# Attention plus a spectral layer on one core: folding the spectral weights by column, and reordering the start of the kernel

## The chip, the core and the metric

The kernel runs on one core of a Trainium2 chip. A core has five engines that run their own instruction queues in order: TensorE (PE, matrix multiply; PEld is its weight load), VectorE (DVE), ScalarE (ACT), GpSimd (POOL) and SyncE (SP, which here only issues DMAs). PE writes to PSUM banks, and DVE or ACT carry results from there to SBUF; POOL works on SBUF alone. The metric is the device time of one launch in microseconds, and lower is better.

## What is computed

For x of shape (2, 2048, 256), with xn = layernorm(x):

```
out = x + attention(xn) + spectral(xn) + bias
attention: q = xn@wq (16 heads of 16), k, v = xn@wk, xn@wv (4 heads), rotary on q and k,
           causal softmax(q k^T / 4) v, then @wo
spectral:  real(ifft(fft(xn) @ (w_re + i w_im)))       along the 256 features
```

The spectral layer is linear in xn, so the kernel works it out as one 256x256 matrix, called mff, and adds xn @ mff. With C and S the cosine and sine tables (dft[0], dft[1]) mff is a sum of products of the form C·(w·C), S·(w·S) and so on, divided by 256.

## The kernel before, in words

Work is cut into 8 blocks n of 512 rows: for each of four row ranges j one block of each of the two batch rows, so that blocks 0 and 1 have j = 0, blocks 2 and 3 have j = 1, and so on. Every block goes through the same chain.

1. `load_x` (L166) loads the block by one 512 KB DMA from SP's queue into one of two buffers xt. Block 0's is issued first, then the rotary table `trig` (L180), then block 1's (L181). The projection weights come by ACT's queue.
2. `row_stats` (L233, DVE, four times), `row_power` (L241, POOL: rstd), `row_shift` (L247, DVE: -mean*rstd), and `norm` (L398), which scales and shifts in place: on DVE for block 0, on POOL for all others.
3. `transpose_x` (L405): PE transposes through a PSUM bank, and ACT copies to xnT. `features` (L419) multiplies by the projection weights, once for keys and values (c = NK) and twice for the queries (c = 0, 1), each time two terms k into one bank, which ACT copies to `raw` (L427). `other_half` gives the swapped halves for the rotary turn.
4. `rotate` and `split` (L514, L531) turn the rows and split them into three bf16 parts, seven operations for each c: on DVE for block 0, on POOL for the others. SP's DMAs then stack the parts into `qst` (queries) and `kst` (keys).
5. For each of the block's four head groups (a "unit"): the exact row maxima, by PE products `sm` and DVE's TENSOR_REDUCE `mx` (L636), the so-called A work; the scores again, transposed, `st` (L743), with ACT's exponential `es` (L745), the B work; and the values `av` (L780), the V work. A unit's scores need its maxima, which `parts` and `spread` (L644, L668) put into `qst` by a small DMA from ACT's queue.
6. `output` (L895) adds xnT @ mff and attT @ wo in a bank, and DVE adds x and the bias.

`rotary_table` (L276) widens the rotary table for a range j by eight DVE operations (L293, tile trx) and turns it by eight PE transposes (L305, ps_tr). `spectral_matrix` (L315) makes mff: four results `left` (two column halves o, for "at" and "et", bank ps_ff), each a sum of four 256-wide products, and two results `right` (bank ps_mff) of four products each, after ACT has negated the sine table (L320). `product` (L151) issues one product as four matmuls, each for 32 columns of the weights; a float32 one shows as eight records. Its inputs are loaded on POOL's queue by `load_late` (L217).

Nothing runs by priority on the chip: each engine takes its instructions in the order in which the program was written out, and that order comes from a planner in the same file (L919 to L1203). It keeps a modelled clock for each engine (`use` and `send` add costs to it), a table `there` of when each value or buffer slot is ready, and lists ("streams") of pieces, each with a first step, a due step, an engine, the things it needs and the slots it takes. A step is one 128-key tile of B work for one unit. The loop at L1096 takes the earliest piece of the other engines while it is due before PE's next, and otherwise picks PE work: A when late, then a forced piece (F: its due step has come), then B, A, V, and a piece that isn't due yet (M) last. A slot in a ring (three PSUM banks "st", three "raw", eight "es", ...) is taken in turn, and work that needs a slot waits until the user three (or eight) turns before has released it.

The start is written by hand (L963 to L977): 48 transposes of an identity keep PE busy (L968, tile idle), DVE fills the constant tiles of block 0, then row_stats, row_power, load_late, row_shift and the ordering of the weights on ACT. `chain` (L979) puts a block's pieces into streams, with first steps taken from when the block's A work is due; within the PE stream the k-th piece of a later block may start at step `s["pe"] + k // 2`.

Of the kernel before, what the change touches and what calls it, by code (L numbers as in the profile page):

```python
# [10 lines left out]
F32 = mybir.dt.float32  # L11
# [6 lines left out]
P = 128  # L18
# [5 lines left out]
def tile_attn_plus_spectral_ffn(  # L24
# [79 lines left out]
    def slot(tag, more=0):  # L104

        return tag, used[tag] + more - ring[tag]
# [57 lines left out]
    xt = {}  # L164

    def load_x(n):  # L166
        send("sp", 512, [slot("xt")], [("xt", "in", n)])
        take_slot("xt")
        xt[n] = work.tile([P, NI, D], F32, tag="xt", bufs=2, name=f"xt{n}")
        nc.sync.dma_start(out=xt[n], in_=block_rows(n))  # L170

    take_slot("qst"), take_slot("qst")
    load_x(0)
# [43 lines left out]
    def load_late():  # L217

        for name, src, tag, bufs in (
            ("wre", w_re, "inv", 2), ("dc", dft[0], "inv", 2),  # L220
            ("wim", w_im, "attT", 2), ("ds", dft[1], "avs", 3),
        ):
            take_slot(tag)
            spec[name] = work.tile([P, NK, D], F32, tag=tag, bufs=bufs, name=name)
            nc.gpsimd.dma_start(out=spec[name], in_=src.rearrange("(c p) n -> p c n", p=P))
            send("pool", 256, (), ["spec"])
        nc.gpsimd.dma_start(out=wo_sb, in_=wo.rearrange("(c p) n -> p c n", p=P))
        nc.gpsimd.dma_start(out=bias_sb, in_=bias.partition_broadcast(P))

# [3 lines left out]
    def row_stats(n, i):  # L233
        if i == 0:
            mv[n] = work.tile([P, NI, 2], F32, tag="mv", bufs=2, name=f"mv{n}")
        st = work.tile([P, 6], F32, tag="bn", bufs=3, name=f"bn{n}_{i}")
        nc.vector.bn_stats(st, xt[n][:, i, :])
        nc.vector.bn_aggr(mv[n][:, i, :], st)
        use("dve", 0.53, [("xt", "in", n)], [("mv", n)])

    def row_power(n):  # L241
        rstd[n] = work.tile([P, NI], F32, tag="rs", bufs=2, name=f"rs{n}")
# [3 lines left out]

    def row_shift(n):  # L247
        shift[n] = work.tile([P, NI], F32, tag="sh", bufs=2, name=f"sh{n}")
        nc.vector.scalar_tensor_tensor(
            shift[n], mv[n][:, :, 0], -1.0, rstd[n], ALU.mult, ALU.mult  # L250
        )
        use("dve", 0.2, [("rs", n)], [("sh", n)])

# [20 lines left out]
    def rotary_table(j):  # L276
        ex = []

        def expand():
            at = []  # L280
            for a in range(2):
                ex.append(work.tile([P, NI, P], F32, tag="raw", bufs=3, name=f"trx{j}_{a}"))
                at.append(slot("raw"))
                take_slot("raw")
            for f in range(2):
                for a, e, k in ((0, 0, 0), (0, 1, 0), (1, 0, 2), (1, 1, 1)):
                    cols = f * HP + e * QD
                    wide = (
                        trig[:, j * NI : (j + 1) * NI, k, :]
                        .unsqueeze(3)  # L290
                        .to_broadcast([P, NI, HALF, NKV])
                    )
                    nc.vector.tensor_reduce(  # L293
                        ex[a][:, :, cols : cols + QD].rearrange("p i (d h) -> p i d h", h=NKV),
                        wide.unsqueeze(4), AX.X, ALU.max,
                    )
            use("dve", 1.15, at, [("trx", j)])
            there["trx slots", j] = used["raw"]

        def turn(a):  # L300
# [9 lines left out]
        return expand, turn  # L310


    mff = const.tile([P, NK, D], F32, name="mff")

    def spectral_matrix():  # L315
        wre, wim, dc, ds_ = (spec[k] for k in ("wre", "wim", "dc", "ds"))
        neg_s = work.tile([P, NK, D], F32, tag="xr", bufs=3, name="neg_s")
        at_ = work.tile([P, NK, D], F32, tag="xr", bufs=3, name="at_")
        et_ = work.tile([P, NK, D], F32, tag="xr", bufs=3, name="et_")
        nc.scalar.mul(neg_s, ds_, -1.0)  # L320
        use("act", 0.48, ["spec"], ["neg_s"])
        first_xr = used["xr"]
        for _ in range(3):
            take_slot("xr")
        pieces = []

        def left(o, name, dst, parts):
            cols = slice(o * P, (o + 1) * P)
            ps = bank(f"ps_ff{o}")[:, :D]
            for a, (w, f) in enumerate(parts):  # L330
                for c in range(NK):
                    product(
                        ps, w[:, c, cols], f[:, c, :],
                        start=(a == 0 and c == 0), stop=(a == 1 and c == NK - 1),
                    )
            nc.scalar.mul(dst[:, o, :], ps, 1.0 / D)
            through_bank(1.87, ["neg_s"], "act", 0.29, [("left", o, name)])

        def right(r):
            cols = slice(r * P, (r + 1) * P)  # L340
            ps = bank(f"ps_mff{r}")[:, :D]
            for a, (w, f) in enumerate(((at_, dc), (et_, neg_s))):
                for c in range(NK):
                    product(
                        ps, w[:, c, cols], f[:, c, :],
                        start=(a == 0 and c == 0), stop=(a == 1 and c == NK - 1),
                    )
            nc.scalar.copy(mff[:, r, :], ps)
            lefts = [("left", o, name) for o in range(NK) for name in ("at", "et")]
            through_bank(1.87, lefts, "act", 0.29, [("mff", r)])  # L350
            if r == NK - 1:
                for tag, k in (
                    ("inv", 0), ("inv", 1), ("attT", 0), ("avs", 0),
                    ("xr", first_xr), ("xr", first_xr + 1), ("xr", first_xr + 2),
                ):
                    there[tag, k] = clock["pe"]

        for o in range(NK):
            pieces.append((["neg_s"], lambda o=o: left(o, "at", at_, ((wre, dc), (wim, ds_)))))
            pieces.append((["neg_s"], lambda o=o: left(o, "et", et_, ((wim, dc), (wre, neg_s)))))  # L360
        lefts = [("left", o, name) for o in range(NK) for name in ("at", "et")]
        for r in range(NK):
            pieces.append((lefts, lambda r=r: right(r)))
        return pieces

# [11 lines left out]
    def project(n):  # L379
# [2 lines left out]
        b, j = blocks[n]  # L382
        e, eng = (nc.vector, "dve") if n == 0 else (nc.gpsimd, "pool")
        MULT, SUB, CAST, NORM = (0.72, 0.72, 0.46, 0.33) if n == 0 else (1.23, 1.13, 0.63, 0.53)
        raw, sw, swp, part, ra, at = {}, {}, {}, {}, {}, {}
        sends = []
        streams.append(sends)

# [27 lines left out]
            if c == NK - 1:  # L416
                there["xt", n] = clock["pe"]

        def features(c):  # L419
            ps = bank(f"ps_q{n}_{c}")  # L420
            for k in range(NK):
                product(
                    ps, wp[:, k, c, :], xnT[n][:, k, :], start=(k == 0), stop=(k == NK - 1)
                )
            raw[c] = work.tile([P, SB], F32, tag="raw", bufs=3, name=f"raw{n}_{c}")
            at[c] = take_slot("raw")
            nc.scalar.copy(raw[c], ps)  # L427
            through_bank(
                1.83, ["wp", *(("xnT", n, k) for k in range(NK))], "act", 0.48, [("raw", "in", n, c)],
                [("raw", at[c] - ring["raw"])],  # L430
            )
            if n >= 2:
                other_half(c)
# [134 lines left out]
        ]  # L568
        for c in (NK, 0, 1):
            table = [("cs", j, 1)] * (n >= 2)  # L570
            pe.append(("pe", ["wp", *table, *xs], ["st", "raw"] + ["sw"] * (n >= 2), lambda c=c: features(c)))
            if n < 2:
                pe.append(("pe", [("raw", "in", n, c)], ["st", "sw"], lambda c=c: other_half(c)))
            if c == NK:
                pe.append(("pe", [("raw", "in", n, NK), ("ones", n)], ["st"], proj_v))
# [397 lines left out]
        row_stats(0, i)  # L973
    row_power(0)
    load_late()
    row_shift(0)
    order_weights()  # L977

    def chain(n, starts, late=0):  # L979

        norms, pe, rot = project(n)
        eng = norms[0][0]
        stats = [("dve", [("xt", "in", n)], [], lambda i=i: row_stats(n, i)) for i in range(NI)]
        stats.append(("pool", [("mv", n)], [], lambda: row_power(n)))
        stats.append(("dve", [("rs", n)], [], lambda: row_shift(n)))
        s = starts
        if n > 1:
            stream([("sp", [], ["xt"], lambda: load_x(n))], s["load"], s["load"])
# [13 lines left out]
                out_rot.append((at, at + late + 2 + k // 2, *p))  # L1002

    def table(j, since):
        expand, turn = rotary_table(j)
        last = [("cs used", at_block[B - 1, j - 2])] if j >= 2 else []
        stream(
            [("dve", last, ["raw", "raw2"], expand)]
            + [("pe", [("trx", j)], ["st"], lambda a=a: turn(a)) for a in range(2)],
            since, since + 3,  # L1010
        )
# [4 lines left out]
    chain(1, early, 1)  # L1016
    load_x_2 = stream([("sp", [], ["xt"], lambda: load_x(2))])

    def spectral():
        for needs, piece in spectral_matrix():  # L1020
            spectral_pieces.append((-1, 8, "pe", needs, ["st"], piece))

    spectral_pieces = stream([("act", ["spec"], [], spectral)], -1, 8)
    for n in range(2, NB):
        at = next(k for k, d in enumerate(due) if d >= a_from[NG * n])
        starts = dict(load=at - 30, stats=at - 24, pe=at - 20, rot=at - 17)
# [228 lines left out]
```

## Time and profile before

| what | us |
|---|---|
| median of 3 runs (925.45 to 928.35) | 925.58 |
| the profiled execution's own time | 926.44 |
| its span, first to last instruction | 924.7 |
| PE busy | 904.6 |
| DVE busy | 748.0 |
| ACT busy | 653.7 |
| POOL busy | 370.1 |

The profile is of one execution. "Busy" is the time in which at least one instruction of the engine ran; a matmul's end is modelled, so PE's figure is somewhat generous. A timeline row gives the start, the time (of several instructions, merged, if it ends in xN), engine, line, operation, tiles and shapes, and in brackets how long the engine had been idle and what released it. The chain is the path of work and waits that ended last. A table by stage gives, for each stretch of time, its length and then the busy time of PE, PEld, DVE, ACT and POOL, with instruction counts, the clock granted to PE (1.00 is full), the share of the DMA engines and GB/s.

### The profile page before, as it was taken

What the parts mean: (1) busy time and instruction counts of PE and PEld (TensorE: products, weight loads), DVE (VectorE), ACT (ScalarE), POOL (GpSimd) and SP (SyncE); (2) the same over time, 40 slices, a digit from 0 to 9 for tenths busy, and PEclk for the clock granted to TensorE, in tenths of its full rate; (3) what the DMA queues carried; (4) which work ended last, traced back from release to release, by engine and by line L of the source; (5) the groups of instructions that cost most, each with busy time, mean ns of one, the idle gap of its engine ahead of it and who ended that gap; (6) DMA issues with size and microseconds to landing.
All of it is one profiled execution on the core that took longest, in us unless ns stands there. A gap on an engine that the chain in (4) does not pass through costs nothing.

```text
span 924.7 us, 38985 instructions
## 1 busy us (share of the span) xinstructions
PE 904.6 (98%) x17324; PEld 500.5 (54%) x17324; DVE 748.0 (81%) x1056; ACT 653.7 (71%) x1375; POOL 370.1 (40%) x556
## 2 busy tenths in 40 slices
PE   7999899999999999999999999999999999999997
PEld 4666565655555555555555555555455554645443
DVE  6878697789789996998995999979789988788601
ACT  3266565587757784888865777857688878588784
POOL 7298666824672424822236520311572021102111
PEclk9999999999999999999999999999999999999999
DMA  5435823341244011440002500010133001100000
GB/s 165 119 90 143 199 92 106 97 132 38 65 121 124 27 38 34 112 129 26 14 27 85 150 28 13 27 60 14 31 109 88 15 3 38 49 14 15 27 1 24
DMA packets 41992, 62.13 MB, mean 67 GB/s; under 512 B 8840, under 2 KB 32120, under 8 KB 41824
## 3 DMA queue, kind: packets, MB, share of 16 engines
q1 hardware_dynamic: 32400, 41.18, 16.5%
q0 software_dynamic: 8128, 17.69, 5.9%
q8 instruction: 135, 2.21, 1.0%
q10 hardware_dynamic: 1296, 0.79, 0.3%
q14 instruction: 33, 0.27, 0.1%
HBM read 32.75 MB, written 18.40 MB: 55 GB/s over the span
## 4 chain that ended last, share of the span: by engine, by line
PE 89%; DVE 5%; ACT 3%; issue 1%; DMA 1%; POOL 1%; ACTq 0%; SPq 0%; DVEq 0%; POOLq 0%
PE av L780 24%; PE st L155 22%; PE sm L155 17%; PE sm L631 7%; PE po L155 6%; PE ps_q L155 4%; DVE mx L636 2%; PE sp L155 2%; PE sm L627 2%; PE st L738 2%; ACT es L745 1%; PE ps_x L411 1%; PE st L734 1%; ACT es L747 1%; PE ps_m L671 0%
## 5 line engine op out<-in xcount | busy, mean ns | idle before, releaser
L636 DVE TENSOR_REDUCE mx<-sm 128x2 f32<-128x1024 f32 (+3 forms) x640 | 648.9, 1057 | 87.4 <-PE sm L631 44.1
L745 ACT ACTIVATE es<-st 128x512 f32<-128x512 f32 (+3 forms) x1194 | 552.4, 543 | 179.2 <-PE st L155 145.6
L155 PE MATMUL st<-qst,kst 115*32 115x512 bf16 (+3 forms) x4264 | 327.2, 354 | 1.1 <-ACT es L745 0.4
L780 PE MATMUL av<-es,va 128*32 128x512 f32 (+3 forms) x2560 | 299.9, 529 | 0.6 <-issue 0.3
L155 PE MATMUL sm<-kst,qst 112*32 112x512 bf16 x3072 | 239.1, 379 | 0.1
L155 PEld LDWEIGHTS <-kst 115*32 115x32 bf16 x4608 | 161.1, 95 | 140.6 <-issue 64.8
L752 POOL TENSOR_SCALAR_AFFINE_SELECT es<-es 128x256 f32<-128x256 f32 x192 | 76.7, 406 | 276.0 <-ACT es L745 234.8
L155 PEld LDWEIGHTS <-qst 112*32 112x32 bf16 x3072 | 96.0, 96 | 93.0 <-issue 64.8
L631 PE MATMUL sm<-kst,qst 112*32 112x32 bf16 (+15 forms) x2048 | 122.3, 281 | 0.3 <-issue 0.3
L627 PE MATMUL sm<-mask,ident_h 128*32 128x128 bf16 (+3 forms) x2048 | 100.2, 201 | 1.8 <-DVE mx L636 1.0
L780 PEld LDWEIGHTS av<-es,va 128*32 128x32 f32 x2560 | 85.1, 109 | 28.6 <-ACT avs L791 2.6
L631 PEld LDWEIGHTS <-qst 112*32 112x32 bf16 x2048 | 66.3, 97 | 34.3 <-issue 20.6
L627 PEld LDWEIGHTS <-ident_h 128*32 128x32 bf16 x2048 | 66.1, 96 | 32.2 <-issue 25.5
L906 DVE TENSOR_TENSOR xr<-po,xr 128x256 f32<-128x256 f32 x36 | 15.2, 424 | 51.5 <-PE po L155 49.5
L803 POOL DMA_DIRECT2D res<-avs x30 | 18.2, 606 | 82.7 <-ACT avs L791 79.9
L155 PE MATMUL ps_q<-xnT,wp 128*32 128x512 f32 x384 | 45.4, 600 | 0.0
L747 ACT ACTIVATE es<-sp 128x1024 f32<-128x1024 f32 (+3 forms) x43 | 36.6, 907 | 7.6 <-PE sp L155 7.4
L427 ACT COPY raw<-ps_q 128x512 f32<-128x512 f32 x24 | 14.1, 585 | 35.0 <-PE ps_q L155 35.0
L518 POOL TENSOR_TENSOR ra<-raw,cs 128x512 f32<-128x512 f32 (+1 forms) x21 | 27.4, 1304 | 24.2 <-ACT raw L427 23.0
L738 PE MATMUL st<-qst,kst 115*32 115x480 bf16 (+15 forms) x512 | 36.8, 284 | 0.1
L155 PE MATMUL po<-wo_sb,attT 128*32 128x256 f32 x512 | 34.4, 379 | 0.7 <-ACT attT L869 0.7
L155 PE MATMUL po<-mff,xnT 128*32 128x256 f32 x512 | 34.4, 380 | 0.0
(108 smaller groups left out, 657.0 us busy)
## 6 DMA issues: line engine op xcount, KB each, us to landing
qst<-run SPq DMA_DIRECT2D x62, 128.0 KB
res<-avs POOLq DMA_DIRECT2D x30, 256.0 KB, 3.0
run<-part SPq DMA_DIRECT2D x31, 192.0 KB
qst<-run SPq DMA_DIRECT2D x31, 192.0 KB
xt<-in_L_attn_x_dram SPq DMA_DIRECT2D x8, 512.0 KB
xr<-in_L_attn_x_dram SPq DMA_DIRECT2D x16, 256.0 KB
out_dram<-xr SPq DMA_DIRECT2D x16, 256.0 KB
sw<-raw SPq DMA_DIRECT2D x60, 64.0 KB
```

Source lines behind the costliest of these rows:

```text
L155: nc.tensor.matmul(to[q : q + QD], lhsT[:, q : q + QD], rhs, start=start, stop=stop)
L518: e.tensor_tensor(ra[c][:r], raw[c][:r], cs[j][:r, 0, :], ALU.mult)
L627: nc.tensor.matmul(to[:, at:wd], ident_h[:, q : q + QD], mask[:, q:], start=True, stop=True, skip_group_check=True,)
L631: nc.tensor.matmul(to[:, : at + QD], rows[:, q : q + QD], keys[:, : at + QD], start=False, stop=True, skip_group_check=True,)
L636: nc.vector.tensor_reduce(t["mx"][:, i, 2 * pr : 2 * pr + 2, k], ps[0][:, :, :wd], AX.X, ALU.max)
L738: nc.tensor.matmul(to[:, at:], keys[:, q : q + QD], rows[:, at:], start=False, stop=True, skip_group_check=True,)
L745: nc.scalar.activation(es[u, t, pr][:, e, lo:], ps[:, lo:], AF.Exp, scale=SCALE)
L747: nc.scalar.activation(es[u, t, pr][:, :, lo:], wide[pr][:, :, lo:], AF.Exp, scale=SCALE)
L752: nc.gpsimd.affine_select(out=es[u, t, pr][:, :, lo : lo + P], in_=es[u, t, pr][:, :, lo : lo + P], pattern=[[0, 2], [1, P]], compare_op=A ...
L780: nc.tensor.matmul(av[u][QD * h : QD * (h + 1), lo:], va[at_block[b, t // NI]][:, t % NI, h, :], es[u, t, h // 2][:, h % 2, lo:], start=(t ...
L803: nc.gpsimd.dma_start(out=res[n, c][f], in_=avs[u])
L906: nc.vector.tensor_tensor(xr[n, r][:, e, :], po, xr[n, r][:, e, :], ALU.add)
```

## The change

- **Loads.** Block 0 is loaded by four DMAs of 128 KB, one for each 128 rows, so that each row_stats waits for its own; other blocks as before.
- **Table.** The widening of the rotary table for j = 0 is issued on DVE between row_stats and row_shift of block 0, where it had come after row_shift.
- **Shift.** row_shift of blocks 1 to 7 goes from one DVE operation to two POOL operations.
- **Spectral weights.** Columns d and 256-d of w_re and w_im are first added or subtracted: six POOL operations ("folds"), four of them over 2x127 elements per partition, the operand for column 256-d read backwards; two copy the columns 0 and 128. Each `left` is then one sum of four products for a column half (issued in two pieces of two products), and each `right` is two products, one of them with a table `half_sb` of cosine row 128 and sine rows 1 to 127, which two more POOL DMAs load into a slot of the "es" ring. ACT's negation is gone.
- **Projections.** `features` is issued in two pieces, one for each k, between which the planner may put other PE work; the bank is held from the first to the copy after the second.
- **Planner's costs.** row_stats 0.53 to 0.6, the widening of the table 1.15 to 1.6.

```
     def load_x(n):
...
+        step = NI if n else 1
+        for i in range(0, NI, step):
+            send("sp", 128 * step, [at], [("xt", "in", n, k) for k in range(i, i + step)])
+            nc.sync.dma_start(out=xt[n][:, i : i + step, :], in_=block_rows(n)[:, i : i + step, :])
...
+        take_slot("es")
+        half_sb = spec["half"] = work.tile([P, D], F32, tag="es", bufs=ES, name="half_sb")
+        nc.gpsimd.dma_start(out=half_sb[0:1], in_=dft[0, P : P + 1, :])
+        nc.gpsimd.dma_start(out=half_sb[1:P], in_=dft[1, 1:P, :])
...
     def row_shift(n):
...
+            nc.gpsimd.tensor_scalar(shift[n], mv[n][:, :, 0], -1.0, None, ALU.mult)
+            nc.gpsimd.tensor_tensor(shift[n], shift[n], rstd[n], ALU.mult)
+            use("pool", 0.4, [("rs", n)], [("sh", n)])
...
     def spectral_matrix():
...
-        nc.scalar.mul(neg_s, ds_, -1.0)
...
+        up, down, far = slice(1, P), slice(D - 1, P, -1), slice(P + 1, D)
...
+        def fold(to, cols, one, two, op, last=False):
+            def go():
+                pool.tensor_tensor(to[:, :, cols], one, two, op)
...
+        def ends_of(to, w):
+            pool.tensor_copy(to[:, :, 0:D:P], w[:, :, 0:D:P])
...
+        folds += [lambda: ends_of(of_c, wre), lambda: ends_of(of_s, wim)]
+        fold(of_c, up, wre[:, :, up], wre[:, :, down], ALU.add)
+        fold(of_s, up, wim[:, :, up], wim[:, :, down], ALU.add)
+        fold(of_c, far, wim[:, :, down], wim[:, :, up], ALU.subtract)
+        fold(of_s, far, wre[:, :, up], wre[:, :, down], ALU.subtract, True)
+
+        def left(o, a):
+            v, f = ((of_c, dc), (of_s, ds_))[a]
...
+            for c in range(NK):
+                product(
+                    ps, v[:, c, o * P : (o + 1) * P], f[:, c, :],
+                    start=(a == 0 and c == 0), stop=(a == 1 and c == NK - 1),
+                )
...
         def right(r):
-            for a, (w, f) in enumerate(((at_, dc), (et_, neg_s))):
-                for c in range(NK):
...
+            for c, f in enumerate((dc[:, 0, :], half_sb)):
+                product(
+                    ps, left_sb[:, c, r * P : (r + 1) * P], f,
+                    start=(c == 0), stop=(c == NK - 1),
+                )
...
-        def features(c):
+        def features(c, k):
+            if k == 0:
+                held[c] = bank(f"ps_q{n}_{c}"), take_slot("st")
+            ps, at_st = held[c]
+            product(ps, wp[:, k, c, :], xnT[n][:, k, :], start=(k == 0), stop=(k == NK - 1))
...
-            pe.append(("pe", ["wp", *table, *xs], ["st", "raw"] + ["sw"] * (n >= 2), lambda c=c: features(c)))
+            pe.append(("pe", ["wp", *table, xs[0]], ["st", "raw"] + ["sw"] * (n >= 2), lambda c=c: features(c, 0)))
+            pe.append(("pe", [xs[1]], [], lambda c=c: features(c, 1)))
...
     row_power(0)
     load_late()
+    table_0 = rotary_table(0)
+    table_0[0]()
     row_shift(0)
     order_weights()
...
-        stats.append(("dve", [("rs", n)], [], lambda: row_shift(n)))
+        stats.append(("pool", [("rs", n)], [], lambda: row_shift(n)))
...
-    spectral_pieces = stream([("act", ["spec"], [], spectral)], -1, 8)
+    folds, products = spectral_matrix()
+    stream([("pool", ["spec"], [], fold) for fold in folds], -1, 4)
+    stream([("pe", *piece) for piece in products], -1, 8)
```

## The prediction, made before the changed kernel ran

> **What bounds the kernel now.** I read the page's engine table first, then a table by stage in steps of 4 us, then the chain, then the timelines of the stage that the change touches.
>
> ```profile
> span 924.7 us, 38985 instructions
> PE 904.6 (98%) x17324; PEld 500.5 (54%) x17324; DVE 748.0 (81%) x1056; ACT 653.7 (71%) x1375; POOL 370.1 (40%) x556
> ```
>
> PE is busy for all but 20.1 us. So the end moves for two reasons only: PE gets less to do, or its idle time changes. The table by stage tells where that idle time lies (second number: PE's busy time of 4.00; third from the end: granted clock):
>
> ```profile
> 8.00:12.00 4.00, 2.09 (x16) 1.48 (x13) 3.02 (x12) 2.47 (x7) 4.00 (x5) 0.97 0.32 88
> 12.00:16.00 4.00, 4.00 (x23) 1.64 (x23) 2.50 (x10) 1.30 (x3) 3.88 (x9) 0.61 0.87 261
> 16.00:20.00 4.00, 3.28 (x32) 0.90 (x28) 2.40 (x4) 0.96 (x2) 3.76 (x8) 1.00 0.43 147
> 20.00:24.00 4.00, 3.29 (x36) 1.02 (x36) 3.76 (x7) 1.16 (x3) 2.75 (x6) 1.00 0.20 67
> ...
> 104.00:108.00 4.00, 1.76 (x55) 1.37 (x58) 1.55 (x2) 1.13 (x5) 3.89 (x4) 0.91 0.37 121
> 108.00:112.00 4.00, 4.00 (x100) 3.35 (x95) 2.85 (x3) 2.11 (x4) 2.13 (x3) 0.66 0.87 233
> ```
>
> About 5 us are lost before 24 us, and 2.2 us in one gap near 105 us. In both places some 3.4 us at half clock follow ((0.03+0.39) x 4 / 0.5 and (0.09+0.34) x 4 / 0.5). The chain, in order of time, shows what PE stands behind (start, time, what):
>
> ```profile
> 29.80 2.76 DMA run<-part
> 32.58 2.74 DMA qst<-run
> 35.33 2.69 POOL xt L399 x5
> 38.06 0.33 PE ps_x L411
> ...
> 104.68 2.19 issue
> ```
>
> Block 1's norm (POOL xt L399) is on the chain, though its data came in the first 10 us. The timelines of POOL and DVE say why:
>
> ```profile
> 8.98 0.16 DVE L249 SCALAR_TENSOR_TENSOR sh<-mv,rs 128x4 f32<-128x4 f32 x1 [1.51 <-POOL rs L244]
> 9.06 1.63 DVE L293 TENSOR_REDUCE trx<-trig 128x128 f32<-128x128 f32 x8
> 18.85 1.26 POOL L244 TENSOR_TENSOR rs<-rs,neg_half 128x4 f32<-128x4 f32 x1
> 33.81 0.15 DVE L249 SCALAR_TENSOR_TENSOR sh<-mv,rs 128x4 f32<-128x4 f32 x1
> 34.78 4.30 POOL L399 TENSOR_SCALAR xt<-xt,rs,sh 128x256 f32<-128x256 f32 x8
> ```
>
> Block 1's rstd is ready at 20.1 us. Its shift stands in DVE's queue behind all of block 0's rotation and block 2's statistics, until 33.8, so the norms of blocks 1 and 2 run at 34.8 to 39.1. Meanwhile PE has the spectral products:
>
> ```profile
> 23.70 1.05 PE L155 MATMUL ps_ff<-dc,wre 128*32 128x256 f32 x16
> 24.56 1.05 PE L155 MATMUL ps_ff<-ds,wim 128*32 128x256 f32 x16
> 35.41 1.13 PE L155 MATMUL ps_mff<-neg_s,et__327 128*32 128x256 f32 x16
> ```
>
> Each row of 16 is two products; from start to start it takes 0.86 us, so a product is 0.43 us.
>
> **The change, part by part.**
>
> *Spectral products.* Before: 6 sums of 4 products, 24 x 0.43 = 10.3 us of PE. After: 2 lefts of 4 and 2 rights of 2, 12 x 0.43 = 5.2 us. PE loses 5.2 us of work, and that is worth 5.2 us only if other work fills the place. In before, nothing could: block 1 was not normed. ACT also loses the negation (0.63) and two copies (0.38 each), which is worth nothing, as ACT is idle there (1.05 us busy of 28 to 32).
>
> *Shift on POOL.* Seven DVE operations of 0.15 us go; 14 small POOL ones come, at 0.24 us each (POOL's 128x4 TENSOR_SCALAR of row_power took 0.23 to 0.24): 0.5 us a block, 3.4 in all, on an engine that is 40% busy. What matters is the queue. POOL's order for block 1 becomes power, shift, norm with nothing of DVE between. Two more DMA issues (0.6 to 0.7 each, like the 0.58 of the bias) push POOL back by 1.3, the earlier start (below) pulls by 0.6: power ends at about 20.8, the shift at 21.3, four norms of 0.55 at 23.5. Block 1 can be transposed 11 to 14 us sooner. That is the filler: two transposes (about 0.6 each for four, by the steps of the chain at 39 to 42), three projections of 1.75, three swaps of 0.9, one value turn of 0.4, together 9.7 us.
>
> *Does PE stay full?* From 21 us on it has the rest of block 0 (about 2), block 1 (9.7), spectral (5.2) and the first two units' maxima (each some 2.6 by the planner's cost; the chain's pieces agree): 22 us, to about 43. The scores began at 48.9 and are then due at about 44: maxima of the first unit begin some 2.5 us sooner and lose the 1.9 us in which DVE waited for PE (8 reductions of mean 0.78 in 8.3 us). So supply and demand match to about 1 us; I count the 5.2 in full and put the failure of this among the rivals.
>
> *Folds.* POOL's 128x512 TENSOR_TENSOR takes 1.30 us (L518), so 254 elements about 0.65; no row shows an operand read backwards, so the bounds are 0.65 and twice that. Two small copies at 0.24. Sum 3.1 to 5.7 us. A rule speaks against their place: GPSIMD Engine Reference, "8. Key points", says in the Trainium skill that POOL shares its SBUF interfaces with VectorE and contends with DVE instructions that have two SBUF inputs, and block 0's rotation on DVE is just that. The row: the pow of row_power took 1.05 us with DVE idle and 1.26 at 18.85 beside such a DVE operation, while DVE's kept its 0.68. By the rule alone I would have to charge DVE's chain up to the folds' 3 us; by the row POOL pays 20% and DVE nothing. I take the row: folds of 0.8, 3.7 us in all, 23.5 to 27.2. POOL was idle from 22.8 to 33.4, so they cost nothing; without that cover they would delay block 1's rotation, which began at 44.5 and has then 14 us of room. Their inputs landed 4.0 us after the last issue at 11.3, before POOL gets there.
>
> *First loads.* Three more issues on SP at 0.5 us push the table's and block 1's DMA from 1.3 and 1.8 to about 2.8 and 3.3. They queue behind block 0's data anyway, which landed at 5.2; bounds 0 and 1.5 for the table, I take 0. The statistics can begin when DVE's memsets end (4.63) and not at 5.25: gain 0.6 at most.
>
> *Table ahead of shift.* DVE waited 1.51 us for POOL's power (row at 8.98), then spent 1.63 on the table, and only then did the norms start (10.61). Afterwards the table runs inside that wait: statistics to 6.9, table to 8.5, shift at 8.6, norms at 8.8. With the 0.6 this is 1.8 us. If the table's data were late, shift and norms would wait behind it, up to 1.5.
>
> *Clock.* PE idled 1.80 us before its first table transpose, and half clock followed. TensorE: Matmul & The Clock Gate, "Why this matters for your kernels", asks only for no idle gaps over about 3 us; by that the half clock does not come from this gap, and closing it saves nothing more. By the rows, gaps of 1.8 and 2.19 us were each followed by it, and the 0.7 us lost in 16 to 20 was not. Afterwards the transposes follow the warm-up with no gap (table ready at 8.5, warm-up to 8.55). I take the row, at 1.0 of the 1.7 us that 3.4 at half clock can cost, as PE partly waits there anyway. Against it 0.5 for a gap near 21 us, where block 1 isn't ready yet. Start in sum: 1.8 + 1.0 - 0.5 = 2.3 us.
>
> *Projections in two pieces.* No instruction is added. The bank is held longer; bounds 0 and the rival below; I take 0, since the planner itself cannot hand out more than two further banks before the second piece. The extra first steps (k // 2 up to 4 for nine pieces, where six gave 2) delay the last projection by two steps, with 12 or more to spare.
>
> **Sum.** 5.2 + 2.3 = 7.5 us off the profiled execution's 926.44: 918.9. That execution lies 0.9 over the median of the runs, so on their scale 918.1.
>
> **Rivals.**
> 1. *The work is not replaced.* PE waits for DVE's maxima between 31 and 44 us, and the start of the scores decides. For: DVE is busy 2.77 to 3.24 of 4 there, and part of the rest was waiting for PE. Against: PE's list above. Only the start's gain is left, 2.5 us: 923.
> 2. *The gap at 104.7 goes too.* It is not a wait that the profile shows: PE stops in the middle of a product. The order behind it shifts, so it may vanish or come elsewhere. Gone, it gives 2.2 + 1.7: 914. The likeliest is that this crowded stage (DMA share 0.9) keeps a gap like it.
> 3. *Slower: a bank held.* In blocks 2 to 7, 18 times, one of three banks stays with a half-done projection. Each time at most two score products then wait for ACT's 0.54 us copies: 1.1 us at worst, 0.75 taken, 13.5 in all: 932. It turns the sign over 0.3% from 0.57 us per hold. Against: ACT itself waited 145.6 us for scores, so it is seldom behind, and PE has other work.
>
> **Chances.** The forecast 0.47, rival 1 0.22, rival 2 0.24, rival 3 0.07. Within 0.3% (2.8 us) is about what a measurement of this kernel can tell from no change. Forecast, rival 2 and a third of rival 1 lie under 922.8: faster 0.79; same 0.14; slower 0.07. The range goes from below rival 2 to above rival 1, 911.5 to 924.
>
> **What would show it.** PE has 96 records fewer of ps_ff and ps_mff together (192 before); norms on DVE start near 8.8; the clock of 12 to 16 us is near 1; block 1's norm on POOL lies near 22 and not 34.8; first scores near 44; PE's idle time up to 44 under 6 us. I am wrong if PE shows gaps between 31 and 44 with the reductions in front of them, if folds take over 1.5 us or lengthen DVE's rotation, if the start of the norms waits for the table's DMA, or if the later stages lose what the first 50 us gained.

## The result, and the profile after

The changed kernel took 928.5 us (median of 22 runs, 926.42 to 932.36), the kernel before in the same comparison 926.38 (22 runs, 922.89 to 930.99): ratio 1.003, 95% interval 1.0019 to 1.0041. The forecast was 918.1. The profiled execution took 929.23 us. A single execution lies within some 5 us of the median, so a ratio below is of medians, and a profile shows where time lies in one execution. Much of this scatter goes with the clock granted to PE: of 130 runs of the kernel before in the comparisons below, the 11 at 1.000 took 923.95 us on average and the 21 at 0.994 took 929.15. The page after:

```profile
span 927.5 us, 38848 instructions
...
PE 901.9 (97%) x17228; PEld 495.2 (53%) x17228; DVE 749.8 (81%) x1049; ACT 653.0 (70%) x1372; POOL 380.7 (41%) x578
```

PE has the 96 records fewer that were forecast. Its busy time fell by 2.7 us and not by 5.2, in part because 3.4 us more of its work ran at half clock (table below), while its idle time (span minus busy) rose from 20.1 to 25.6. The table by stage tells where (columns as before; third from the end is the clock):

```profile
12.00:16.00 4.00, 3.29 (x32) 0.90 (x28) 1.92 (x5) 0.96 (x2) 3.94 (x9) 1.00 0.85 265
20.00:24.00 4.00, 1.73 (x16) 0.16 (x8) 3.76 (x7) 0.58 (x1) 3.85 (x7) 1.00 0.30 101
24.00:28.00 4.00, 1.42 (x3) 0.54 (x3) 3.84 (x5) 0.00 (x0) 3.83 (x8) 0.70 0.35 107
28.00:32.00 4.00, 3.54 (x17) 1.52 (x21) 3.42 (x8) 1.17 (x2) 3.83 (x6) 0.50 0.63 146
...
116.00:120.00 4.00, 2.73 (x64) 1.97 (x67) 1.04 (x2) 2.26 (x7) 3.10 (x7) 0.72 0.93 234
```

The half clock of 12 to 16 us is gone, as forecast. In its place stands a hole from 20 to 32 us: PE idles 2.27 + 2.58 + 0.46 = 5.3 us there (1.0 before), and half clock follows. A gap near 116 us remains. The chain of the changed kernel, in order of time, says what PE stands behind in the hole; where the chain of before had block 0's DMAs and then block 1's norm at 35.33, it now has POOL alone:

```profile
21.77 2.37 POOL kst L413 x4
24.14 0.08 issue
24.22 0.60 POOL sh L264
24.90 0.20 POOL sh L265
25.10 0.14 POOL vc L353
25.24 3.18 POOL xt L436 x4
28.46 1.33 PE ps_x L448 x5
29.79 3.18 PE ps_q L155 x16
```

L413 fills the constant tiles of block 3 (`ones`), which a run below could fill at 62.64 us instead without harm. They stand between block 1's rstd and its shift. PE's timeline from the same stretch:

```profile
21.37 1.06 PE L155 MATMUL ps_sw<-raw,swap 128*32 128x512 f32 x8 [0.70 <-ACT raw L466]
25.83 0.47 PE L448 MATMUL ps_x<-ident,xt 128*128 128x128 f32 x1 [3.39 <-POOL xt L436]
...
29.72 3.25 PE L155 MATMUL ps_q<-xnT,wp 128*32 128x512 f32 x16
...
33.66 0.22 PE L667 MATMUL sm<-mask,ident_h 128*32 128x128 bf16 x4
```

PE waits 3.39 us for the first norm of block 1, then runs the transposes and a projection at half clock (3.25 us for 16 records, 1.9 at full). The first maxima `sm` stand behind them in PE's queue and start at 33.66 (31.46 before), although block 0's rotation on DVE was over at 29.96, sooner than before (31.12). The first scores start at 49.96 (48.81 before, 44 forecast).

Over the profiled executions, PE's idle time and its time at half clock in the first 144 us (the second counts half) give the sum:

| kernel | idle | half clock | idle + half/2 |
|---|---|---|---|
| before | 10.4 | 6.8 | 13.8 |
| after | 15.9 | 10.2 | 21.0 |

That is 7.2 us more of waiting against 5.2 us less of work: 2.0 slower. The medians say 2.1, these two profiled executions differ by 2.8. All runs together point the same way: their mean granted clock was 0.9967 for the kernel before (the 130 runs above) and 0.9947 for the changed one (22 runs). As an estimate from these, 0.0020 x 926 = 1.9 us more went to half clock, while the work taken away about paid for the added idle time.

### The profile page after: what moved, and what is told of

It reads as the page before. It is cut to its first block, busy times and chain, and to the rows that moved or that the text cites. A ratio compares the mean times of both kernels' runs of the same rounds, so it can differ in the third digit from the quotient of the medians.

```text
span 927.5 us, 38848 instructions
## 1 busy us (share of the span) xinstructions
PE 901.9 (97%) x17228; PEld 495.2 (53%) x17228; DVE 749.8 (81%) x1049; ACT 653.0 (70%) x1372; POOL 380.7 (41%) x578
## 4 chain that ended last, share of the span: by engine, by line
PE 87%; ACT 4%; POOL 4%; issue 2%; DMA 2%; DVE 1%; ACTq 0%; SPq 0%; POOLq 0%
PE av L820 24%; PE st L155 23%; PE sm L155 18%; PE sm L671 6%; PE po L155 6%; PE ps_q L155 4%; ACT es L785 3%; PE sp L155 2%; PE sm L667 1%; PE ps_x L448 1%; ACT es L787 1%; POOL kst L413 1%; DMA inv<-sums 1%; PE st L778 1%; PE st L774 1%
## 5 line engine op out<-in xcount | busy, mean ns | idle before, releaser
L155 PE MATMUL st<-qst,kst 115*32 115x512 bf16 (+3 forms) x4264 | 331.0, 354 | 1.6 <-ACT es L785 0.7
L671 PE MATMUL sm<-kst,qst 112*32 112x160 bf16 (+15 forms) x2048 | 120.7, 280 | 1.3 <-issue 1.3
L667 PE MATMUL sm<-mask,ident_h 128*32 128x64 bf16 (+3 forms) x2048 | 99.1, 201 | 0.7 <-DVE mx L676 0.2
L155 PE MATMUL ps_q<-xnT,wp 128*32 128x512 f32 x384 | 49.7, 609 | 0.2 <-ACT xnT L451 0.2
L778 PE MATMUL st<-qst,kst 115*32 115x64 bf16 (+15 forms) x512 | 36.6, 285 | 0.7 <-issue 0.4
L774 PE MATMUL st<-mask_t,ident_h 128*32 128x96 bf16 (+3 forms) x512 | 30.6, 204 | 4.8 <-ACT es L785 3.7
```

Source lines behind the costliest of these rows:

```text
L155: nc.tensor.matmul(to[q : q + QD], lhsT[:, q : q + QD], rhs, start=start, stop=stop)
L667: nc.tensor.matmul(to[:, at:wd], ident_h[:, q : q + QD], mask[:, q:], start=True, stop=True, skip_group_check=True,)
L671: nc.tensor.matmul(to[:, : at + QD], rows[:, q : q + QD], keys[:, : at + QD], start=False, stop=True, skip_group_check=True,)
L774: nc.tensor.matmul(to[:, lo : at + QD], ident_h[:, q : q + QD], mask_t[:, : q + QD], start=True, stop=True, skip_group_check=True,)
L778: nc.tensor.matmul(to[:, at:], keys[:, q : q + QD], rows[:, at:], start=False, stop=True, skip_group_check=True,)
```

## The experiments

**Theory A:** POOL's time ahead of block 1's norm holds PE, and the removed products were filler. Rivals: split projections hold a bank (B in the first expectations); the time is set by the first maxima plus a constant (D); PE's work is paid in full wherever it lies (E). Where a later expectation uses letters anew, it says for what. Ratios are to before.

**POOL's queue.** First, the five memsets of block 3 get a later first step, in the planner:

```
-        starts["ones"] = 0 if n < 4 else 8 * n - 26
+        starts["ones"] = 0 if n < 3 else (4 if n == 3 else 8 * n - 26)
```

> The changed kernel with one edit: block 3's constant tiles (2.9 us of POOL memsets) may be written only from step 4 on, so POOL's queue for block 1 becomes power, shift, norm without them. Theory A (start: PE starves from 22 to 28 us behind POOL, then runs at half clock, and that eats the 5.2 us saved): block 1's norm ends near 25.5 and not 28.4, PE's idle time between 20 and 32 us falls from 5.3 to some 2.5 us, and the time falls by 3 us or more against the changed kernel: ratio to before about 1.000 or less. Theory B (later stages: banks held by half-done projections, other gaps after 60 us): the start gets better but the time stays at 1.003.

Measured: 924.37 us, ratio 0.9983 (0.9972 to 0.9993). One line turns a loss into a small gain: this version beat both kernels, the one before by 1.7 us, in one comparison that was not repeated. The order of PE's work changed with it, so POOL's time was not yet shown. The same with block 2's memsets later too (`{2: 2, 3: 4}.get(n, 8 * n - 26)`):

> As the previous one, and block 2's constant tiles also wait (until step 2), so that power, shift, norm and folds of POOL come 5 us sooner than in the changed kernel. Theory A: norm ends near 20 to 22 us, folds near 25, no idle stretch of PE over 2 us before 44 us, no half clock between 24 and 34, first scores near 45 instead of 50, time 5 to 7 us under the changed kernel: ratio 0.995 to 0.998. Theory B: 1.002 to 1.003. A third one (C: POOL beside DVE slows DVE's rotation of block 0) lets the rotation end later, near 31, and gives back about 1 us.

Measured: 929.46, ratio 1.0038 (1.0022 to 1.0055). Block 1's norm now began at 19.51, 5.7 us sooner than in the changed kernel, and the time did not fall. POOL went straight on with folds and block 1's rotation beside block 0's rotation on DVE. In this run's timeline of DVE, and its table by stage:

```profile
29.23 1.65 DVE L587 TENSOR_TENSOR rb<-raw,part 128x512 f32<-128x512 f32 x1
```

```profile
32.00:36.00 4.00, 0.59 (x16) 0.26 (x12) 3.83 (x12) 0.22 (x1) 2.54 (x5) 0.82 0.55 145
```

The operation takes 0.69 us alone. The last third of the rotation took 8.33 us, 4.40 before. PE ran dry at 32 to 36 us, waiting for the first maximum, which DVE took up after the rotation and block 2's statistics:

```profile
35.83 0.27 PE L667 MATMUL sm<-mask,ident_h 128*32 128x128 bf16 x4 [3.41 <-DVE mx L676]
```

Sooner is no gain when the engine that is freed then slows the one that PE waits for next. (The order of PE's and POOL's work changed in this run, so how much each part of it costs is not shown.)

To show POOL's time alone, two runs kept the order of every other engine's instructions exactly as in the changed kernel. One takes the memsets of block 3 out of `ones` (into a function `fill`) and issues them behind block 3's norm:

```
+            if n == 3 and i == NI - 1:
+                fill(3, nc.gpsimd)
```

> The changed kernel with one thing moved and every engine's order otherwise frozen: block 3's five POOL memsets (2.94 us at 21.19 to 24.13) stand behind block 3's own norm instead of ahead of block 1's shift. PE's, ACT's, DVE's and SP's instructions stand exactly as in the changed kernel. Theory A (POOL's time ahead of block 1's norm is what holds PE): shift at about 21.3, norm over at about 25.5, first transpose of block 1 near 23, PE's idle time before 32 us down from 8.5 to about 6, first unit's maxima out about 2.5 us sooner (44), time about 2 to 3 us under the changed kernel's, ratio to before about 1.000. Rival B (the gain of the earlier run with these memsets later came from the new order of PE's work, not from POOL's time): time as the changed kernel's, ratio 1.003.

The other adds five memsets ahead of the shift:

```
+            for _ in range(5 if n == 1 else 0):
+                nc.gpsimd.memset(va[3], 1.0)
```

> The changed kernel with five more POOL memsets of 128x512 (0.53 us each, 2.65 us) ahead of block 1's shift, rewriting ones that are already there; all other instructions of all engines stand in the same order. Theory A: block 1's norm, its transposes and the first unit's maxima come about 2.6 us later (49.1), PE's idle time before 32 us rises by about 2.6 and the half clock lasts longer, time 931 to 932, ratio about 1.006. Rival B (the time ahead of the first scores is made up later, since DVE and ACT are idle for parts of it): 1.003 as the changed kernel.

Measured: 927.67, ratio 1.0001 (0.9986 to 1.0015), and 932.07, ratio 1.0052 (1.0033 to 1.007). PE's first transposes of block 1 with the memsets moved, and with the dose:

```profile
23.47 0.33 PE L454 MATMUL ps_x<-ident,xt 128*128 128x128 f32 x1 [0.71 <-POOL xt L440]
```

```profile
29.20 2.94 PE L450 MATMUL ps_x<-ident,xt 128*128 128x128 f32 x8 [6.30 <-POOL xt L438]
```

| kernel | shift on POOL | first `sm` | ratio |
|---|---|---|---|
| memsets moved | 21.30 | 31.24 | 1.0001 |
| changed kernel | 24.22 | 33.66 | 1.003 |
| five more | 27.33 | 35.80 | 1.0052 |

2.9 us less of POOL gives 2.7 us (0.0029 x 926), 3.1 more costs 2.0. The second is hardly clear of noise by itself, but these two runs stood in one comparison, and there 6.0 us of POOL cost 4.4 (932.07 against 927.67). With the order frozen both ways, the first half of theory A is shown: POOL's time ahead of the norm holds PE, at 0.65 to 0.9 us per us.

Shift back on DVE, in the changed kernel:

```
+        stats.append(("dve", [("rs", n)], [], lambda: row_shift(n)))
```

> The changed kernel with the shift of blocks 1 to 7 back on DVE, where block 1's stands behind block 0's rotation and block 2's statistics; all else as in the changed kernel. Forecast of the prediction (the shift on POOL is what lets block 1 in): block 1's norm at about 34, PE without filler between 23 and 31 but for the spectral products (5.2 us), idle time before 32 us above 8.5, 2 to 5 us slower than the changed kernel, ratio 1.005 to 1.008. Rival (as with the shift alone, 1.001: it gives nothing, because POOL's norm then also lies beside DVE's rotation): block 0's rotation is over near 28.5 without POOL's norm beside it, scores begin at about 31, ratio 1.000 to 1.003.

Measured: 932.39, ratio 1.005 (1.003 to 1.0069): the moved shift is worth about 2 us inside the change, the low end of what its theory said, and hardly clear of noise (the changed kernel's interval ends at 1.0041). Block 1's norm lay at 33.90 again, and PE waited 3.22 us for the folds instead. The shift alone on the kernel before:

> The kernel before with only the shift of blocks 1 to 7 on POOL. Theory A: block 1's work comes 10 us sooner, with the spectral products still there PE is full from 21 us on, but more filler stands in front of the first unit's products and POOL's norms lie beside DVE's rotation (about 1 us longer): the first maxima no sooner than 44.3, ratio 0.999 to 1.003. If an earlier block 1 were worth its full move, 0.995.

Measured: 927.01, ratio 1.001 (0.9991 to 1.0028): nothing. Telling the planner the measured POOL costs (norm 0.82, shift 1.0, fold 0.85), on the version with 0.9983:

> The best kernel so far with the planner told what POOL was measured to take at the start: 1.75 for block 1's power, 1.0 for its shift (0.5 for later blocks), 0.82 for its norm, 0.85 for a fold. Only the order changes: scores of the first unit ahead of the swap of block 1's keys, two steps of B work elsewhere between 50 and 70 us. Theory (the order made from wrong costs loses 1 to 3 us): PE's idle time before 48 us falls from 6.4 to 5 or less, ratio 0.996. Rival (the order of the start does not matter beyond the first maxima): 0.998 as that kernel's.

Measured: 926.95, ratio 0.9997 (0.9981 to 1.0013). PE's idle time before 48 us was 6.6 and not 5. That the wrong costs lose the rest is not supported.

**Spectral products.** The changed kernel with the old products (24, ACT's negation, no folds):

> The changed kernel with the spectral weights as before: 24 products, no folds, no half_sb loads; loads, table, shift and projections as changed. Theory A: the 10.3 us of products stand ready from 21 us on without POOL and fill PE where the changed kernel starves, so PE's idle time up to 40 us is near the 5.3 of before less 2, and the time is no worse than the changed kernel's in spite of 5.2 us more work: ratio 0.998 to 1.003. If folding is worth its 5.2 us of PE in full, this kernel is 5 us slower than the changed one: ratio 1.008.

Measured: 928.59, ratio 1.003 (1.0015 to 1.0044). It has 5.2 us more of PE work and the same time, within some 1.7 us: in the changed kernel the folding is worth nothing that these runs can tell, since the old products fill the hole (PE idled 1.9 us in 20 to 32, not 5.3):

```profile
20.00:24.00 4.00, 3.98 (x56) 1.49 (x48) 3.83 (x7) 0.97 (x2) 3.67 (x8) 1.00 0.29 96
24.00:28.00 4.00, 2.09 (x12) 1.10 (x16) 3.79 (x6) 0.98 (x2) 2.60 (x4) 1.00 0.32 103
28.00:32.00 4.00, 4.00 (x88) 1.88 (x80) 3.41 (x11) 1.07 (x3) 1.27 (x1) 1.00 0.52 136
```

With the hole went half clock: the mean granted clock is 0.9967 here and 0.9947 in the changed kernel, so of the 5.2 us some 1.9 went to half clock there (an estimate from these two) and the rest, by difference, to idle time. This supports the second half of theory A, though PE's order is not the same in the two kernels.

The old products once the queue is mended, to be read against 0.9983:

> The best kernel so far (changed kernel with block 3's constant tiles from step 4) with the spectral products as before: six sums of four products, ACT's negation, no folds and no half_sb, so 5.2 us more PE work and about 5.4 us less POOL work beside block 0's rotation. Theory A (removed products were filler ahead of the first maxima, and the folds cost DVE's rotation 1.4 us): ratio 0.997 to 0.999, no slower than that kernel, rotation of block 0 over near 29 and not 30. Rival (the folding is worth its PE time once POOL's queue is mended): 5.2 us slower than that kernel, ratio about 1.004.

Measured: 928.54, ratio 1.0007 (0.9988 to 1.0025). Between theory and rival: there the folding is worth about 2.2 us (0.0024 x 926, uncertain by some 2) of 5.2. Folds alone on the kernel before:

> The kernel before with only the folded spectral weights. The forecast's own step: 5.2 us of PE work less, worth 5.2 if PE is full, ratio 0.995. Theory A: the products wait for POOL's folds (ready near 27) where they could start at 23.3 before; block 1 is still normed at 35 or later, so PE starves between 23 and 38, the 5.2 us become idle time and, with a half clock, the time is that of before or up to 2 us more: ratio 1.000 to 1.003.

Measured: 940.07, ratio 1.0143 (1.0111 to 1.0175), outside both expectations. The planner answers by norming block 2 first and block 1 only at 49.22; block 1's projections and rotation then come behind scores, and DVE has nothing to reduce. Columns 3 to 5 of the table are PE, PEld and DVE; folds alone first, then before:

```profile
76.00:80.00 4.00, 3.42 (x105) 2.03 (x105) 0.00 (x0) 3.33 (x12) 3.81 (x5) 1.00 0.64 182
80.00:84.00 4.00, 3.28 (x104) 1.79 (x104) 0.57 (x2) 3.62 (x10) 3.80 (x4) 1.00 1.05 260
```

```profile
76.00:80.00 4.00, 3.81 (x144) 2.97 (x147) 3.85 (x5) 3.77 (x11) 3.35 (x4) 1.00 0.75 199
```

So filler has a second side: when block 1 is late, maxima for its units are late 40 us on. The run that made it late on purpose (`chain(1, dict(early, pe=1), 1)` on the 0.9983 version) agrees:

> The kernel of the first experiment (block 3's constant tiles later), and block 1's PE pieces may start only from step 1 on, so that before the first scores PE has block 0, the spectral products and the first maxima alone. Theory D (the end is the first maxima's time plus a constant 880.5 us, as in the five profiles so far): the first maxima leave near 39, and the time falls by another 3 us, ratio 0.995. Theory E (after the first scores PE is the bound, so work pushed behind them is paid in full): 9.7 us of block 1 come behind, up to 3 are won in front: 3 to 7 us slower than the first experiment, ratio 1.002 to 1.006.

Measured: 938.46, ratio 1.014 (1.0109 to 1.017), though its first maxima left ACT at 42.51 us, as in the 0.9983 version (42.18). Theory D is refuted by this. E had the direction but neither the size (14.1 us slower than the 0.9983 version, 3 to 7 expected) nor the place: DVE was idle 25 us between 60 and 100 us (7.6 before).

Folds on DVE, on the 0.9983 version:

> The best kernel so far with the six folds on DVE instead of POOL; the planner puts them among the first unit's maxima, near 36 us, and the spectral products behind. Theory of contention[...] (DVE's rotation of block 0 takes 5.87 us for its last third beside the folds and 4.4 without): that third is back at about 4.5 us, first scores up to 1.4 us sooner, but DVE has about 2.5 us of folds to do among the maxima; ratio 0.998 to 1.000. Rival (the length of the rotation comes from block 0's own data and not from POOL): that third stays near 5.9 us, and the time is later by the folds' 2.5 us, ratio 1.001.

Measured: 934.07, ratio 1.0059 (1.0039 to 1.008). Both expectations missed the size: the rotation's last third fell from 5.87 to 4.74 us, so the lengthening does come from POOL; but the products then came at 61 us, PE had no filler and ran at half clock for 10 us, until about 35. Next, contention alone: the run with memsets moved, each wide fold replaced by memsets, which leaves the weights out of mff.

```
-                pool.tensor_tensor(to[:, :, cols], one, two, op)
+                pool.memset(to, 1.0 / D)
+                pool.memset(to[:, 0, :], 1.0 / D)
```

> The frozen-order run with block 3's memsets moved, and in it each of the four wide folds replaced by two POOL memsets of the same tile (128x512 and 128x256, about 0.8 us together), so that POOL is as long busy beside block 0's rotation but reads nothing. The spectral matrix is then made of constants and not of the weights. All other instructions of all engines stand in the same order. Theory of contention (DVE's two-input operations are lengthened by POOL's two-input ones; memsets did not lengthen them): the last third of block 0's rotation falls from 6.4 us (24.05 to 30.4) to about 4.9 (the norms still lie beside its first part), first scores about 1.3 us sooner, time 0.5 to 1.3 us under that run's, ratio about 0.999. Rival (the rotation's end is not on the path, PE has block 1's projections and the products until then): rotation shorter, time as that run's, ratio 1.000.

Measured: 927.38, ratio 0.9996 (0.9981 to 1.0011), against 1.0001 with the folds. DVE's timeline with folds, then with memsets:

```profile
27.47 1.09 DVE L593 TENSOR_TENSOR rb<-raw,part 128x512 f32<-128x512 f32 x1
...
29.37 1.09 DVE L601 TENSOR_TENSOR part<-rb,part 128x512 bf16<-128x512 f32 x1
```

```profile
27.28 0.69 DVE L594 TENSOR_TENSOR rb<-raw,part 128x512 f32<-128x512 f32 x1
...
28.64 0.69 DVE L602 TENSOR_TENSOR part<-rb,part 128x512 bf16<-128x512 f32 x1
```

The rotation was over 1.1 us sooner, and the first `sm` stood at 31.28 instead of 31.24: PE's queue has a projection and a product ahead of it. The contention is real and, in this order, costs nothing that the medians can tell.

**The other two parts.** Projections in one piece, in the changed kernel:

> The changed kernel with each projection in one piece again. Theory A: the start is the same within 1 us and the ratio stays at 1.002 to 1.004. Theory B (banks held between the pieces): idle time of PE after 60 us falls by 3 us or more and the ratio falls to 0.999 or less.

Measured: 929.92, ratio 1.0041 (1.0025 to 1.0058): not better, so nothing shows that the two pieces lose a bank, and theory B falls. Loads and table alone on the kernel before:

> The kernel before with only the loads in four pieces, the table ahead of the shift, and the two planner costs that belong to them. Theory A (what counts is how PE is fed up to the first scores, and the first unit's maxima set when the scores start): block 0's norms start near 8.6 as in the changed kernel, no half clock at 12 us, all of block 0 some 2.5 us sooner, POOL is not used beside the rotation: the first unit's maxima leave for the queries near 42 instead of 44.3 and the time falls by 2 to 2.5 us, ratio 0.997 to 0.998. Theory B (the start does not matter): 0.999 to 1.001.

Measured: 926.43, ratio 0.9996 (0.9979 to 1.0014). First maxima left ACT 2.18 us sooner (42.09, 44.27 before), and the median kept 0.4 of it (a gain of 1.9 to a loss of 1.3). In the profiled execution the lead was 3.5 us when the eighth unit's values were copied (132.20, 135.73 before) and 1.5 at the last unit's. The mean granted clock rose from 0.9967 to 0.9987, by estimate 1.9 us less at half clock, so what is lost again is not clock. Where it goes is not settled.

## Why the prediction was wrong, step by step

- *Start.* Right in place: statistics from 4.67, norms from 8.60 (8.8 forecast), table transposes at 8.51 with no gap, full clock in 12 to 16. The size was off: 2.3 us forecast, 0.4 measured alone (1.9 at most).
- *Shift on POOL: "power, shift, norm with nothing of DVE between".* This step failed. Nothing of DVE stands between, but POOL's own work does. Forecast: shift from 20.8, norms over at 23.5. Measured: 24.22 and 28.41. It was to be seen in the timeline of POOL before, right behind the row that the prediction quotes at 18.85:

```profile
19.86 0.69 POOL L373 MEMSET va<- 128x512 f32 x1
20.61 2.20 POOL L376 MEMSET kst<- 32x512 bf16 x4
```

The prediction used "POOL was idle from 22.8" and did not ask what ended at 22.8. The planner puts them first because it holds the shift for ready 0.12 us after POOL's clock and takes what can start first, within 0.1. Cost shown: 2.7 us, by the run with the memsets moved.
- *Sizes on POOL.* A norm took 0.80 instead of 0.55, beside DVE's rotation (0.54 at 34.78 before), the shift 0.9 instead of 0.5, both ahead of block 1's projections: another 1.4 us late (4 x 0.25 + 0.4).
- *Does PE stay full?* This failed with the queue. PE was to be full from 21 us on, and all 5.2 us of the products were counted; their worth was 0 in the changed kernel and about 2.2 with the queue mended. (The list of block 1's work adds up to 9.55 and not 9.7, which changes nothing.) Rival 1 had the right mechanism for this but the wrong place (31 to 44 us), and no rival let the early hole grow.
- *Folds.* Sizes held within the bounds: 0.72, 1.17, 0.64 and 0.73, with 0.37 and 0.18 for the copies, 3.8 in sum (3.7 forecast). The rule of the Trainium skill (GPSIMD Engine Reference, "8. Key points") that POOL contends with DVE instructions of two SBUF inputs was set aside on the row of an operation of four elements. The runs side with the rule: DVE's 0.69 became 1.09 beside folds and stayed 0.69 beside memsets. It costs nothing in the run that isolates it, and the rotation's last third was 3.9 us longer in the run that moved more POOL work there.
- *Clock.* Forecast 1.0 us for closing the gap ahead of the table's transposes; half clock there is gone, and the run of loads and table alone spent by estimate 1.9 us less at half clock. But the row was no rule. Folds alone and shift alone start as before did, and their profiles have full clock in 12 to 16: the warm-up ran longer there, and the gap was 1.11 and 0.79 us instead of 1.80. Later in shift alone PE stood still for as long as in the row, and no half clock followed:

```profile
93.49 0.23 PE L743 MATMUL st<-qst,kst 115*32 115x160 bf16 x1 [1.84 <-issue]
```

```profile
92.00:96.00 4.00, 2.46 (x93) 1.75 (x93) 2.68 (x6) 1.68 (x5) 2.26 (x3) 1.00 0.60 186
96.00:100.00 4.00, 3.73 (x137) 2.81 (x135) 3.39 (x4) 3.21 (x9) 2.69 (x4) 1.00 0.48 153
```

The rule of some 3 us in the Trainium skill (TensorE: Matmul & The Clock Gate, "Why this matters for your kernels") fares no better: a gap of 3.14 us (folds alone) was followed by none, and waits of at most 0.71 us (memsets moved) by one of 3.41 us. So half clock in one profile is not a fixed cost of the kernel.
- *Rival 3, the held bank.* Rightly small: the run in one piece shows no cost. *Rival 2, the gap at 104.7*, did not vanish: it stands near 116.

The miss in the profiled execution is 2.8 + 7.5 = 10.3 us. Products 5.2, memsets 2.7 and start 1.9 make 9.8; each is uncertain by 1.5 to 2, and they overlap where less filler lengthens the same hole.

## What to carry to other kernels

When work moves to another engine's in-order queue, read that queue's timeline around the new place, and ask for every row there whether it must stand ahead; what is idle "from" some time was busy until then. Work taken from a full engine is worth its time only if the engine stays full: PE's redundant products stood exactly where it had nothing else. A planner reacts to a cost or a first step with a new order, so test a suspected delay with the order frozen, by taking it away and by doubling it.

## What the runs showed of the hardware

- In the first 150 us of all 17 profiles the stretches at half clock last 3.41, 6.83 or 10.24 us, that is one, two or three times 3.41. Their number does not follow from one gap's length: the single gaps of PE over 3 us were 6.30 (five more memsets), 4.70 (block 1 late), 4.47 (folds replaced by memsets), 3.41 (both blocks' memsets later), 3.39 (changed kernel), 3.22 (shift back on DVE), 3.14 (folds alone) and 3.08 us (one piece), and with them went three, two, one, two, two, one, none and two. With the memsets moved, one followed waits of 0.70, 0.71, 0.63 and 0.64 us near 25 us. What decides is not settled here.
- POOL's memsets leave DVE's TENSOR_TENSOR at 0.69 us, though a CAST of DVE beside them can take 0.60 to 0.84 instead of 0.43. POOL's TENSOR_TENSOR and TENSOR_SCALAR do lengthen it: DVE's operations of 0.69 took 0.86 to 0.95 beside norms, mostly 1.01 to 1.24 beside folds, and up to 1.65 beside POOL's rotation, which itself took up to 1.71 instead of 1.3. The product that reads one operand from PSUM kept its 0.68 beside norms and folds; in the run with both blocks' memsets later, two of DVE's operations beside folds:

```profile
25.01 1.03 DVE L557 TENSOR_TENSOR ra<-raw,cs 128x512 f32<-128x512 f32 x1
25.96 0.68 DVE L560 TENSOR_TENSOR sw<-ps_sw,cs 128x512 f32<-128x512 f32 x1
```

- A POOL operand read backwards (128x254) took 0.63 to 0.72 with DVE idle; by the 1.30 for 512 elements 0.65 was due, so the extra is under 0.1.
